# Ten samples' x leave SBUF in layer 1 of a two-layer network; their places take weights of the experts early

## The chip, the cores and the metric

The kernel runs on one core of one Trainium2 chip. The metric is the device time of one execution in microseconds (us), as the median of several runs.

## What is computed

A network of two layers works on x of shape (16, 128, 32, 32), float32: 16 samples, 128 channels, 1024 tokens (pixels). The second layer, around which the change lies, is cut here to what matters:

```
x = x + t_ffn0                          # the end of layer 0: its second residual
x = x + conv_block(_ln_c(x))            # two 3x3 convolutions, relu, residual
t = _to_tokens(x)
u = _ln_t(t)                            # (16, 1024, 128)
logits = einsum('bsd,ed->bse', u, gate_w) + gate_b        # 64 experts
probs  = softmax(logits, axis=1)                          # over the tokens
vals, idx = top_k(probs.transpose(0, 2, 1), 8)            # 8 tokens per expert
pooled = sum over the 8 of gathered u * vals              # (16, 64, 128)
h   = gelu(concat(pooled, 1) @ weight1)                   # per expert, (16, 512)
out = concat(h, 1) @ weight2                              # per expert, (16, 128)
t   = t + scatter_add(out * vals)                         # back to the tokens
```

The experts' weights are 64 matrices of 128 x 512 and 64 of 512 x 128 (and a row of bias each), 33.5 MB in all. SBUF holds only a part of them at a time.

## The kernel before, in words

The kernel first runs layer 0. At its end every sample's x lies in DRAM (`xd[b]`, 512 KB each, written at L634), and the long convolution's spectrum lies in DRAM as `yd`, in two pieces: `yd[0]` with 112 rows and `yd[1]` with 16. The last ones of `yd` are written by `finish` (L828 to L835): four tensor operations on GpSimd (POOL), for the very last on VectorE (DVE), and then the stores on SyncE (SP).

**Layer 1, per sample.** `load(b)` brings x (L974) and the two pieces of y (L977). For sample 0, x and the long piece of y go through POOL's queue, as does the long piece for sample 1; all the others go through SP's. Then class `Routed` has one method for each step: `even`, `odd_t` and so on make z of y; `inverse` (L1074) is a TensorE matmul group that turns y and z back into tokens; `add` (L1081) adds it to x; `tokens`, `stats`, `norm` are the layer norm; `terms`, `image`, `conv` and so on are the two convolutions as a Winograd-like scheme (L958 is the matmul line); `last` (L1219) adds their result to x, in place; `tokens2` transposes x for the second norm; then `logits`, `largest`, `exp`, `replace`, `gates`, `turn`, `pool`, `pooled` are the gating, done once for a pair of samples. `gates` stores the pair's gates in DRAM (`gd`, L1290).

**What sets the order.** A table gives for each step its engine, a cost, a due time, what it needs and which buffers it opens and closes. The function `planned` turns the table into one order of (sample, step). The program emits the steps in this order under `manual_schedule`, with the order pinned on all engines and on SP's queue too. An engine, and SP's queue, works strictly in its order: an instruction that has to wait holds up all behind it on the same engine. y has two buffers, so the y load of a sample waits for the `inverse` of the sample two before.

**Places in SBUF.** Pools are stacked. x of all 16 samples stays in SBUF during layer 1, from the load until the output. Each x is a tile of 4 KB per partition with a tag of its own: x0 in pool `xpool2`, x1 to x15 in `xpool3`.

**The experts.** The weights come in 32 halves of 1 MB: half 2g is the first matrix of the four experts of group g, half 2g+1 the second. `load_half(h)` (L904 ff., the DMAs are L915 for even h and L919 for odd) puts half h into a place of `RING`, a list of nine buffers that layer 1 has finished with (y, wi, z, y, cw0, v, cw1, p1, yo). The first nine halves are issued during the last sample's steps: four behind `inverse`, one behind `convc`, four behind `last`. The gates of the pairs come back from DRAM behind them (L1433, seven loads). Then a loop runs over 16 groups: `hidden(g)` (matmuls L1482 with the weights and L1489 with the bias, GELU on ScalarE (ACT) L1494), `turn` (transposes L1502), `output(g)` (matmuls L1513), `collect` (transpose L1524). Behind `hidden(g)` half 2g+9 is issued, and behind `output(g-1)` half 2g+8: each takes the place of the half that has just been used. In the trace TensorE's instructions of the loop are named by what they write: ph (L1482 and L1489), pht, peo, pot.

**The end.** `big` (L1550), `ob` (L1554), and then for each pair, in the order 0, 1, 2, 3, 7, 4, 5, 6: matmuls pfy (L1572), the add to x (on DVE L1582; for every second sample of the odd pairs a copy on ACT L1579 and the add on POOL L1580), and the store to the output (L1583, 16 stores on SP's queue).

**DMA lanes.** A DMA of SP's queue signals one of eight semaphores in turn; before a DMA is issued, SP also waits for the one eight before it, where it doesn't know yet that it has landed.

Of the kernel before, what the change touches and what calls it, by code (L numbers as in the profile page):

```python
# [8 lines left out]
F32 = mybir.dt.float32  # L9
# [5 lines left out]
P = 128  # L15
B, C, H, W = 16, 128, 32, 32
N = H * W
# [32 lines left out]
E, HID = 64, 512  # L50
# [4 lines left out]
EG = 4  # L55
# [14 lines left out]
def metaformer_kernel(ctx: ExitStack, tc: tile.TileContext, io: dict, out: bass.AP):  # L70
    nc = tc.nc
# [22 lines left out]
    xt = {}  # L94
# [3 lines left out]
    for n, (g_, b_, m_, v_) in enumerate(((V_G1, V_B1, V_M1, V_V1), (V_G2, V_B2, V_M2, V_V2))):  # L98
# [15 lines left out]
                name=nc.get_next_instruction_name(), ins=[], outs=[], act_func_set_id=EXP_LN  # L114
# [52 lines left out]
    with ExitStack() as l0:  # L167
        lconst = l0.enter_context(tc.tile_pool(name="lconst", bufs=1))
        l0.enter_context(tc.issue_after(functions.ins))
        xd = [dram.tile([P, N], F32, name=f"xd{b}", tag=f"xd{b}") for b in range(B)]  # L170
# [23 lines left out]
        for i in range(NF):  # L194
            h = hard[:, i : i + 1]
# [15 lines left out]
        with ExitStack() as a0:  # L211
            aconst = a0.enter_context(tc.tile_pool(name="aconst", bufs=1))
            setup = a0.enter_context(tc.tile_pool(name="setup", bufs=2))
            work = a0.enter_context(tc.tile_pool(name="awork", bufs=2))
# [3 lines left out]
            xpool = a0.enter_context(tc.tile_pool(name="xpool", bufs=8))  # L218
# [85 lines left out]
            def load(b):  # L304
                xt[b] = xpool.tile([P, N], F32, name=f"x{b}", tag="x")
                nc.sync.dma_start(xt[b], xs[b])

            for b in range(2):
                load(b)
# [34 lines left out]
            class Attention:  # L344
# [10 lines left out]
                def tokens(self):  # L355
                    if self.b + 2 < B:
                        load(self.b + 2)
                    self.x = xt[self.b]
                    self.pt = big().rearrange("p (j c) -> p j c", c=C)
                    transpose_in(self.pt, self.x)  # L360
# [384 lines left out]
            samples, setting, preparing = {}, filters(), prepare()  # L745
            with tc.manual_schedule(engines=PINNED):
                for p in range(-reach, B):
                    next(preparing, None)
                    for name, d in period:
                        b = p + d  # L750
# [11 lines left out]
        with ExitStack() as g0:  # L762
# [32 lines left out]
            def collect(c, q, pg):  # L795

                for r in range(RG):
                    dst = gs[c].rearrange("p w (g q i) -> p g q w i", g=RG, q=NB)[:, r, q]
                    src = pg[r].rearrange("p i w -> p w i")
                    if r % 2 and (r == 1 or q % 2 or c == 0):  # L800
                        nc.vector.tensor_copy(dst, src)  # L801
                    else:
                        nc.scalar.copy(dst, src)  # L803
# [87 lines left out]
    with ExitStack() as c1:  # L891

        cconst = c1.enter_context(tc.tile_pool(name="cconst", bufs=1))
        first = c1.enter_context(tc.tile_pool(name="cfirst", bufs=1))
        xpool = [c1.enter_context(tc.tile_pool(name=f"xpool{i}", bufs=1)) for i in (2, 3)]
        work = c1.enter_context(tc.tile_pool(name="cwork", bufs=2))
        cps = c1.enter_context(ExitStack())
        ps = cps.enter_context(tc.tile_pool(name="cps", bufs=2, space=PSUM))

        RING = ("y", "wi", "z", "y", "cw0", "v", "cw1", "p1", "yo")
        FIRST = ("wi", "v", "cw0", "cw1", "p1", "y")
        halves = {}  # L904

        def load_half(h):

            g, n = divmod(h, 2)
            if g >= E // EG:
                return  # L910
            es, tag = slice(g * EG, (g + 1) * EG), RING[h % len(RING)]
            pool = first if tag in FIRST else work
            w = pool.tile([P, EG * HID], F32, name=f"we{n}", tag=tag, bufs=RING.count(tag))
            if n == 0:
                nc.sync.dma_start(  # L915
                    w.rearrange("p (e h) -> p e h", e=EG), w1[es, 0:C, :].rearrange("e d h -> d e h")
                )
            else:
                nc.sync.dma_start(  # L919
                    w.rearrange("p (e i) -> p e i", e=EG),  # L920
                    w2[es, 0:HID, :].rearrange("e (p c) o -> p e (c o)", c=NHC),
                )
            halves[h] = w

        wi = first.tile([P, NQ, 2, P], F32, name="wi", tag="wi")
# [41 lines left out]
        def tokens(t):  # L967
            return t.rearrange("p (j c) -> p j c", c=C)

        yts = {}  # L970

        def load(b):
            xt[b] = xpool[b > 0].tile([P, N], F32, name=f"x{b}", tag=f"x{b}")
            (nc.sync if b else nc.gpsimd).dma_start(xt[b], xd[b])  # L974
            yts[b] = first.tile([P, 2, 2 * NM, C], F32, name="y", tag="y", bufs=2)
            for i, js in enumerate((slice(P - 2 * JL), slice(P - 2 * JL, P))):
                (nc.gpsimd if b < 2 and i == 0 else nc.sync).dma_start(  # L977
                    yts[b][js].rearrange("p r x e -> p r (x e)"),
                    yd[i][:, :, b].rearrange("j r x e -> j r (x e)"),
                )  # L980
# [450 lines left out]
        def load_gates(pr, tag, bufs):  # L1431
            gates[pr] = work.tile([P, N], F32, name=f"gt{pr}", tag=tag, bufs=bufs)
            nc.sync.dma_start(gates[pr], gd[pr])  # L1433
# [5 lines left out]
        with tc.manual_schedule(engines=PINNED | {mybir.EngineType.SP}):  # L1439
            for b in range(2):  # L1440
                load(b)
            for n in range(2):
                nc.sync.dma_start(cw[n], cwd[n])
            nc.sync.dma_start(b1, w1[:, C, :])
            for j in range(2):
                nc.sync.dma_start(b2[j * E : (j + 1) * E, :], w2[:, HID, :])
            samples = [None] * B
            for b, name in order:
                if name == "yin":
                    if b > 1:  # L1450
                        load(b)
                    continue
                if samples[b] is None:
                    samples[b] = Routed(b)
                arg = args.get(name, (name,))
                getattr(samples[b], arg[0])(*(
                    getattr(samples[b], a) if a in ("va", "vb") else a for a in arg[1:]
                ))
                if b == B - 1 and name == "inverse":
                    for h in range(4):  # L1460
                        load_half(h)
                elif b == B - 1 and name == "convc":
                    load_half(4)
                elif b == B - 1 and name == "last":
                    for h in range(5, len(RING)):
                        load_half(h)
                elif b == B - 1 and name == "logits":
                    for pr in range(2):
                        load_gates(pr, "tk", 2)
                    for pr in range(2, 4):  # L1470
                        load_gates(pr, "tt", 4)
# [5 lines left out]
        def hidden(g):  # L1477
            w1t = halves[2 * g].rearrange("p (e h) -> p e h", e=EG)
            ph = ps.tile([P, HID], F32, name="ph", tag="big", bufs=2)
            for i in range(EG):  # L1480
                e = g * EG + i
                nc.tensor.matmul(  # L1482
                    ph[i * CG : (i + 1) * CG, :],
                    pooled[:, e : e + 2, :].rearrange("p e b -> p (e b)"), w1t[:, i, :],
                    start=True, stop=False, skip_group_check=True,
                )
            for i in range(EG):
                e = g * EG + i
                nc.tensor.matmul(  # L1489
                    ph[i * CG : (i + 1) * CG, :], ident[0:E, e : e + 1].to_broadcast([E, CG]), b1,  # L1490
                    start=False, stop=True, skip_group_check=True,
                )
            hs = work.tile([P, HID], F32, name="hs", tag="sa")
            nc.scalar.activation(hs, ph, AF.Gelu)  # L1494
            return hs
# [11 lines left out]
        def output(g, ht):  # L1507
            w2t = halves[2 * g + 1].rearrange("p (e c o) -> p e c o", e=EG, c=NHC)
            po = ps.tile([P, C], F32, name="peo", tag="cv", bufs=3)
            for c in range(NHC):  # L1510
                for i in range(EG):
                    cg = slice(i * CG, (i + 1) * CG)
                    nc.tensor.matmul(  # L1513
                        po[cg, :], ht[:, c, cg], w2t[:, i, c, :],
                        start=(c == 0), stop=(c == NHC - 1), skip_group_check=True,
                    )
            og = work.tile([P, C], F32, name="og", tag="pl", bufs=1)
            nc.vector.tensor_copy(og, po)
            return og
# [10 lines left out]
        with tc.manual_schedule(engines=PINNED):  # L1530
# [4 lines left out]
            for g in range(ng + 1):  # L1535
                if g:
                    ht = turn(hs.pop(g - 1))
                if g < ng:
                    hs[g] = hidden(g)
                    load_half(2 * g + len(RING))  # L1540
                if g > 1:
                    collect(g - 2, og.pop(g - 2))
                if g:
                    og[g - 1] = output(g - 1, ht)
                    load_half(2 * g - 1 + len(RING))
            collect(ng - 1, og.pop(ng - 1))
# [17 lines left out]
        with tc.manual_schedule(engines=PINNED):  # L1564
            yt = first.tile([P, 2, N], F32, name="yt", tag="v")
            for pr in (0, 1, 2, 3, 7, 4, 5, 6):
# [8 lines left out]
                for j in range(2):  # L1575
                    b = 2 * pr + j
# [162 lines left out]
```

## Time and profile before

| | |
|---|---|
| median of 3 runs | 1273.64 us (1272.99 to 1274.5) |
| the profiled execution, its own time | 1271.01 us |
| its span, first to last record | 1269.2 us |
| mean granted TensorE clock in the span | 0.967 |
| TensorE busy | 1149.1 us, 91% |
| VectorE busy | 936.2 us, 74% |
| ScalarE busy | 725.9 us, 57% |
| GpSimd busy | 605.3 us, 48% |
| moved by DMA | 164.64 MB, mean 130 GB/s |
| first inverse of layer 1 (L1074) | at 673.79 us |
| last `last` of layer 1 (L1219, sample 15) | at 1129.87 us |
| first matmul of the experts (L1482) | at 1159.08 us |
| first matmul of the end (pfy, L1572) | at 1240.36 us |
| first output store issued (L1583) | at 1244.59 us |

How to read it: times within the profile count from the start of the span. A busy share is an average over stages with different limits, so the table gives the places of the stages too. SP isn't in the busy list: it only issues DMAs. The duration of a DMA line of SP or POOL is the time of issuing; the transfer itself runs later on the 16 DMA engines, which are shared by all queues. In a timeline row the bracket at the end is the engine's idle time before the row and what ended it. In a table of stretches the columns are: stretch, its length, busy time and count of PE, PEld, DVE, ACT and POOL, the TensorE clock, the DMA engines' mean busy share, and GB/s. PE is TensorE's matmuls, PEld its weight loads.

### The profile page before, as it was taken

To read this page: it belongs to the slowest core of one execution; us is meant where nothing else is said; L and a number is where in the kernel's file an instruction comes from. 1 tells how busy PE (TensorE), PEld (TensorE's weight loads), DVE (VectorE), ACT (ScalarE), POOL (GpSimd) and SP (SyncE) were. 2 spreads that over 40 slices of the span, in tenths; PEclk is the share of its full clock that TensorE was granted. 3 is DMA by queue.
4 is the path that set the end of the run, shared out by engine and by line. 5 is a ranking of instruction groups with operands and counts; after the bars stand their busy time and mean duration, and the time that the engine had idled before them with its cause. 6 is when DMAs were issued, how large, how long until landed. Compare 5 with 4: busy or idle time off the path is not lost. (4 is left out here: it accounts for less than half of the span.)

```text
span 1269.2 us, 34025 instructions
## 1 busy us (share of the span) xinstructions
PE 1149.1 (91%) x14244; PEld 934.4 (74%) x14244; DVE 936.2 (74%) x1944; ACT 725.9 (57%) x1420; POOL 605.3 (48%) x801
## 2 busy tenths in 40 slices
PE   4889999999997999999976999999999999977975
PEld 3677777777776998888865888888898888853432
DVE  5788888888765777776765798889898888772325
ACT  4777777767654777777742354565565556542111
POOL 2335545565666688888863444333353442210002
PEclk9999999999998999999998999999999999985998
DMA  7105343443345244444458231213222212055976
GB/s 264 33 30 165 117 139 124 134 158 111 106 134 183 87 136 137 137 136 136 130 196 244 72 81 34 83 34 84 67 55 77 70 50 101 27 190 190 389 285 265
DMA packets 88346, 164.64 MB, mean 130 GB/s; under 512 B 5632, under 2 KB 41728, under 8 KB 87552
## 3 DMA queue, kind: packets, MB, share of 16 engines
q1 hardware_dynamic: 87312, 159.05, 38.6%
q0 software_dynamic: 880, 3.41, 0.8%
q8 instruction: 112, 1.84, 0.6%
q14 instruction: 42, 0.34, 0.1%
HBM read 105.03 MB, written 57.41 MB: 128 GB/s over the span
## 5 line engine op out<-in xcount | busy, mean ns | idle before, releaser
L958 PE MATMUL pcv<-v,cw 128*128 128x256 f32 x1152 | 259.7, 381 | 0.7 <-POOL v L1144 0.7
L958 PEld LDWEIGHTS pcv<-v,cw 128*128 128x128 f32 x1152 | 215.9, 191 | 34.3 <-issue 4.9
L801 DVE COPY g<-pg 128x512 f32<-128x512 f32 x196 | 127.8, 682 | 77.1 <-PE pg L790 77.1
L803 ACT COPY g<-pg 128x512 f32<-128x512 f32 x316 | 161.2, 605 | 31.7 <-PE pg L790 30.9
L790 PE MATMUL pg<-ph,mst 32*128 32x128 f32 x4096 | 139.6, 278 | 5.0 <-issue 3.5
L790 PEld LDWEIGHTS pg<-ph,mst 32*128 32x128 f32 x4096 | 126.0, 186 | 19.1 <-issue 12.4
L814 PE MATMUL py<-g,v 128*32 128x128 f32 x4096 | 127.9, 276 | 8.5 <-POOL v L781 5.7
L814 PEld LDWEIGHTS py<-g,v 128*32 128x32 f32 x4096 | 110.1, 111 | 18.3 <-POOL v L781 5.8
L144 ACT ACTIVATE tok<-tok,sts 128x128 f32<-128x128 f32 x256 | 101.9, 480 | 16.8 <-DVE sts L1031 13.4
L135 DVE BATCH_NORM_STATS2 bst<-big 128x6 f32<-128x256 f32 x256 | 91.1, 416 | 23.3 <-PE big L152 14.1
L781 POOL TENSOR_TENSOR v<-xc 128x256 f32<-128x256 f32 x128 | 99.8, 803 | 8.9 <-DMA xd<-x 8.9
L626 PE MATMUL big<-u,mu 128*128 128x128 f32 (+4 forms) x384 | 86.0, 380 | 0.0
L1144 POOL TENSOR_TENSOR v<-abss 128x256 f32<-128x256 f32 x64 | 49.1, 788 | 66.1 <-DVE abss L1140 54.3
L277 POOL TENSOR_TENSOR xf<-ab 128x256 f32<-128x256 f32 x34 | 24.8, 729 | 112.3 <-DVE ab L244 112.3
L1163 POOL TENSOR_TENSOR yo<-abss 128x256 f32<-128x256 f32 x32 | 23.5, 736 | 109.1 <-DVE abss L1159 109.1
L626 PEld LDWEIGHTS big<-u,mu 128*128 128x128 f32 x384 | 56.7, 191 | 18.0 <-issue 15.4
L875 ACT COPY yt<-py 128x512 f32<-128x512 f32 x64 | 37.5, 586 | 48.9 <-PE py L814 26.4
L1580 POOL TENSOR_TENSOR x<-yt,x 128x1024 f32<-128x1024 f32 x4 | 9.4, 2359 | 115.2 <-ACT yt L1579 115.2
L559 PE MATMUL big<-wf,ub 128*128 128x256 f32 x256 | 62.0, 385 | 0.2
L144 ACT ACTIVATE tt<-tt,sts 128x128 f32<-128x128 f32 x128 | 51.1, 481 | 14.6 <-DVE sts L1031 14.6
L152 PEld LDWEIGHTS big<-ident,x 128*128 128x128 f32 x384 | 46.0, 146 | 17.7 <-issue 10.5
L782 POOL TENSOR_SCALAR v<-v 128x256 f32<-128x256 f32 x64 | 55.2, 862 | 5.6
(247 smaller groups left out, 2480.5 us busy)
## 6 DMA issues: line engine op xcount, KB each, us to landing
we<-in_weight SPq DMA_DIRECT2D x32, 1024.0 KB, 9.9
vd<-xf SPq DMA_DIRECT2D x16, 1024.0 KB, 5.1
xc<-vd SPq DMA_DIRECT2D x64, 256.0 KB, 3.2
yd<-ys SPq DMA_DIRECT2D x32, 512.0 KB, 4.0
y<-yd SPq DMA_DIRECT2D x14, 896.0 KB, 6.7
x<-in_x SPq DMA_DIRECT2D x16, 512.0 KB, 4.6
mi<-in_M_phi SPq DMA_DIRECT2D x16, 512.0 KB, 4.7
xd<-x SPq DMA_DIRECT2D x16, 512.0 KB, 6.1
```

The source lines that it names most:

```text
L135: nc.vector.bn_stats(bst[:, j : j + 2, :].rearrange("p j s -> p (j s)"), src[:, j : j + 2, :].rearrange("p j c -> p c j"),)
L144: nc.scalar.activation(dst[:, j, :], src[:, j, :], AF.Identity, bias=nm[:, j : j + 1], scale=r[:, j : j + 1],)
L559: nc.tensor.matmul(dst, self.ub[:, q, :], wf[:, q, :], start=True, stop=True)
L626: nc.tensor.matmul(self.pa[:, a:hi], mu[:, NF - 1 - si, tap, :], self.u[:, a - tap : hi - tap], start=(tap == 0), stop=(tap == KU - 1),)
L781: nc.gpsimd.tensor_tensor(vv[:, x, 1:, bs], e, o, op)
L782: nc.gpsimd.tensor_scalar(v[:, :, 0, bs], v[:, :, 2, bs], -1.0, None, ALU.mult)
L790: nc.tensor.matmul(pg[r][:, i], mst[rs, 4 * q + i, :], ph[rs, c, :], start=True, stop=True,)
L801: nc.vector.tensor_copy(dst, src)
L803: nc.scalar.copy(dst, src)
L814: nc.tensor.matmul(py[rows, x, kl, :], v[:, (x * NM + m) * JL + jl, 1 - ri : 3 - ri, :] .rearrange("p k b -> p (k b)"), g[:, ((x * 2 + ri) ...
L958: nc.tensor.matmul(pc[:, i], wt[:, dy, k, :], v[:, k, dy * WT : dy * WT + HT], start=(dy == 0), stop=(dy == 2),)
L1144: nc.gpsimd.tensor_tensor(v[:, k, WT : WT + HT], self.ab[:, 0], self.ab[:, 1], op)
```

## The change

x of two samples becomes one tile: `xp0` to `xp7`, 8 KB per partition, all in the pool `xpool2`. The x of pairs 1 to 5 (samples 2 to 11) no longer stays in SBUF: behind `tokens2` of each of these samples x is stored to its place in DRAM, `xd[b]`, through SP's queue. The ring gets five more places, `xp1` to `xp5`, ahead of the nine old ones. Halves 0 to 4 go into them: half 0 is issued behind `tokens2` of sample 4, half 1 behind that of sample 6, and so on to half 4 behind that of sample 12. The nine old places take halves 5 to 13 at the same points of the last sample as before. In the experts' loop half 2g+14 is issued behind `hidden(g)` and half 2g+13 behind `output(g-1)`. When the 32 halves have all been issued, the next five calls of `load_half` bring the ten samples' x back from DRAM, a pair at a time, into the places that come next in the ring; the end then adds to these tiles and stores them.

```diff
-        xpool = [c1.enter_context(tc.tile_pool(name=f"xpool{i}", bufs=1)) for i in (2, 3)]
+        xpool = c1.enter_context(tc.tile_pool(name="xpool2", bufs=1))
...
-        RING = ("y", "wi", "z", "y", "cw0", "v", "cw1", "p1", "yo")
+        AWAY = range(1, 6)
+        RING = tuple(f"xp{pr}" for pr in AWAY) + (
+            "y", "wi", "z", "y", "cw0", "v", "cw1", "p1", "yo",
+        )
...
             g, n = divmod(h, 2)
+            es, tag = slice(g * EG, (g + 1) * EG), RING[h % len(RING)]
             if g >= E // EG:
+                pr = AWAY[0] + h - 2 * (E // EG)
+                if pr in AWAY:
+                    tag = RING[(pr - AWAY[0] + 18) % len(RING)]
+                    pool = first if tag in FIRST else xpool if tag[:2] == "xp" else work
+                    x = pool.tile([P, 2, N], F32, name=f"xb{pr}", tag=tag, bufs=RING.count(tag))
+                    for j in range(2):
+                        xt[2 * pr + j] = x[:, j]
+                        nc.sync.dma_start(x[:, j], xd[2 * pr + j])
                 return
...
         def load(b):
-            xt[b] = xpool[b > 0].tile([P, N], F32, name=f"x{b}", tag=f"x{b}")
+            if b % 2 == 0:
+                xp[b // 2] = xpool.tile([P, 2, N], F32, name=f"xp{b // 2}", tag=f"xp{b // 2}")
+            xt[b] = xp[b // 2][:, b % 2]
             (nc.sync if b else nc.gpsimd).dma_start(xt[b], xd[b])
...
+                if name == "tokens2":
+                    if b // 2 in AWAY:
+                        nc.sync.dma_start(xd[b], samples[b].x)
+                    if b % 2 == 0 and b // 2 - 1 in AWAY:
+                        load_half(b // 2 - 1 - AWAY[0])
                 if b == B - 1 and name == "inverse":
-                    for h in range(4):
+                    for h in range(5, 9):
                         load_half(h)
                 elif b == B - 1 and name == "convc":
-                    load_half(4)
+                    load_half(9)
                 elif b == B - 1 and name == "last":
-                    for h in range(5, len(RING)):
+                    for h in range(10, len(RING)):
                         load_half(h)
```

More of the change, by code (lines that the diff above doesn't have):

```diff
@@ L908, in load_half @@
             g, n = divmod(h, 2)
+            es, tag = slice(g * EG, (g + 1) * EG), RING[h % len(RING)]
             if g >= E // EG:
+                pr = AWAY[0] + h - 2 * (E // EG)
[6 more added lines that the diff above has]
+                        nc.sync.dma_start(x[:, j], xd[2 * pr + j])
                 return
-            es, tag = slice(g * EG, (g + 1) * EG), RING[h % len(RING)]
-            pool = first if tag in FIRST else work
+            pool = first if tag in FIRST else xpool if tag[:2] == "xp" else work
             w = pool.tile([P, EG * HID], F32, name=f"we{n}", tag=tag, bufs=RING.count(tag))
@@ L968, in tokens @@
             return t.rearrange("p (j c) -> p j c", c=C)
-        yts = {}
+        yts, xp = {}, {}
         def load(b):
-            xt[b] = xpool[b > 0].tile([P, N], F32, name=f"x{b}", tag=f"x{b}")
+            if b % 2 == 0:
+                xp[b // 2] = xpool.tile([P, 2, N], F32, name=f"xp{b // 2}", tag=f"xp{b // 2}")
+            xt[b] = xp[b // 2][:, b % 2]
             (nc.sync if b else nc.gpsimd).dma_start(xt[b], xd[b])
```

## The prediction

> **What bounds the kernel now.** I first read the slices of the page, for the stretch in which the weights move:
>
> ```profile
> PE   4889999999997999999976999999999999977975
> ...
> PEclk9999999999998999999998999999999999985998
> DMA  7105343443345244444458231213222212055976
> ```
>
> A slice is 31.7 us. From 760 to 1100 us (slices 24 to 34) TensorE is busy in nine tenths and the DMA engines in one to three: layer 1 is bound by TensorE and leaves the DMA nearly free. In the last slices this turns round. Next the chain of waits, for the experts (from 1159 us):
>
> ```profile
> 1199.74 0.99 PE ph L1482 x8
> 1200.74 13.77 DMA we<-in_weight
> ...
> 1216.11 13.81 DMA we<-in_weight
> 1229.92 0.04 issue
> 1229.96 1.06 PE ph L1482 x8
> ```
>
> Up to 1200 us the chain is TensorE's, then weight loads. TensorE's timeline shows what that costs (start, duration; in brackets the idle time before):
>
> ```profile
> 1195.73 1.06 PE L1482 MATMUL ph<-we,pooled 128*32 128x512 f32 x8
> 1199.67 1.06 PE L1482 MATMUL ph<-we,pooled 128*32 128x512 f32 x8
> ...
> 1209.17 1.06 PE L1482 MATMUL ph<-we,pooled 128*32 128x512 f32 x8 [1.35 <-DMA we<-in_weight]
> 1214.55 1.06 PE L1482 MATMUL ph<-we,pooled 128*32 128x512 f32 x8 [1.38 <-DMA we<-in_weight]
> 1219.53 1.06 PE L1482 MATMUL ph<-we,pooled 128*32 128x512 f32 x8 [0.98 <-DMA we<-in_weight]
> 1224.83 1.06 PE L1482 MATMUL ph<-we,pooled 128*32 128x512 f32 x8 [1.29 <-DMA we<-in_weight]
> 1229.96 1.06 PE L1482 MATMUL ph<-we,pooled 128*32 128x512 f32 x8 [1.13 <-DMA we<-in_weight]
> ```
>
> One group of four experts takes 3.94 us while TensorE is full (the steps 1176.05, 1179.98 ... 1199.67: 23.62 us for six). The last six, from 1199.67 to 1229.96, take 30.29 us. The loads cost 30.29 - 23.62 = 6.67 us. Last, the stretches of 5 us behind it (busy times of PE, PEld, DVE, ACT, POOL; clock; DMA share; GB/s):
>
> ```profile
> 1215.00:1220.00 5.00, 4.02 (x59) 1.82 (x53) 1.26 (x3) 0.60 (x1) 0.00 (x0) 1.00 1.05 408
> 1225.00:1230.00 5.00, 3.87 (x57) 1.70 (x51) 1.26 (x3) 0.60 (x1) 0.00 (x0) 1.00 0.72 276
> 1230.00:1235.00 5.00, 4.33 (x63) 2.10 (x67) 1.43 (x4) 0.60 (x1) 0.00 (x0) 1.00 0.01 2
> 1235.00:1240.00 5.00, 2.26 (x41) 1.56 (x32) 2.41 (x10) 0.00 (x0) 0.00 (x0) 1.00 0.00 0
> 1240.00:1245.00 5.00, 4.64 (x14) 2.06 (x16) 1.98 (x4) 0.00 (x0) 0.00 (x0) 0.66 0.00 0
> 1255.00:1260.00 5.00, 2.72 (x12) 0.94 (x8) 3.91 (x4) 1.01 (x1) 3.76 (x2) 1.00 1.02 419
> ```
>
> The DMA engines are full up to the last weight, idle from 1230 to 1245 us, then full again with the 16 outputs (8.4 MB at 419 GB/s, 20 us). So the end is three limits in a row: weights by DMA, the rest of the experts by TensorE (10.4 us from the last ph at 1229.96 to the first pfy at 1240.36), outputs by DMA (28.9 us from there to the end of the span).
>
> [...] what the tail moves takes its bytes over about 0.40 MB per us. [...] every added DMA holds SP's queue until its wait is met. [...] SP's timeline has such gaps (27.4 us ahead of L919). [...] the gaps here are at most 1.4 us and the clock stays 1.00, so ending them buys the gaps alone.
>
> **The change, part by part.** I compared the built order of both kernels. PE, DVE and ACT keep their order; two waits on weights fall away on PE early and two later. New are ten stores, five early weight halves, ten reloads, and one wait on POOL.
>
> *Five halves early.* In the stage from 1161 us on, 23 halves were loaded; now 18, as 14 instead of 9 lie ready. A half is 1.05 MB, 2.62 us at 0.40 MB/us. The releases are the old ones, so loads start at the same time. Counted in MB units from 1161 us the new queue is 18 weights and five pairs of x: 23 again, so its end stays near 1229.9 us. Half 30, for the last ph, is the 16th: 1229.9 - 7 x 2.62 = 1211.6, needed at 1199.67 + 23.62 = 1223.3. Half 31 is the 19th: 1219.4, needed near 1228 (its peo stands 4.8 us behind that ph). Nothing is late; TensorE keeps 3.94 us to the end. **-6.67 us.** What is late next is TensorE itself, then the outputs.
>
> *Ten reloads of x* (5.24 MB, 13.1 us of DMA). The SP queue has pair 1 ahead of half 31, pairs 3, 2, 5, 4 behind it. Their places come free by about 1211 us (ph of the twelfth group, peo of the eleventh). They end near 1230; the first pfy moves to 1233.7 and the first add, 3.0 us behind it, to 1236.7. They fill the DMA's old idle time: **0**, margin 6.8 us. Without that cover up to 13.1 us. Outputs wait for stores and DMAs long landed.
>
> *Ten stores of x and five loads in layer 1* (10.5 MB). Each store waits on SP for `last` of its sample (L1219, 16 of them, 1.97 us). In SP's timeline the queue's next item is a y load that waits anyway for the inverse of two samples before. For sample 3: last ends at 820.7 us, behind the store stands x of sample 9 (issued at 814.25, needed only at its add some 80 us later) and then y at 837.7. For sample 4: 846.1, next the gates' store at 858.6. The pattern repeats every 56 us; the last one, sample 11 at 1045.0, stands ahead of a weight load of 1036.7, a delay of 8.3 us for something needed near 1178. An even y loaded at 812.5 is first read at 840.6, so DMA contention has 20 us of room; the DMA share there is 0.13 to 0.32. A load's wait for two stores is met: the later was issued 25 us ahead. **0**; a bound from above is 10 issues of 1.75 us (the median of the old xd stores), 17.5 us, if nothing hid them, but SP is idle there for most of the time.
>
> *POOL's x0 load.* x0 now shares a tile with x1, whose place comes free with the last matmul of layer 0 (L814, ends 657.52). Before:
>
> ```profile
> 652.92 0.61 POOL L974 DMA_DIRECT2D x<-xd  x1
> 653.56 1.29 POOL L829 TENSOR_TENSOR ys<-ys 128x512 f32<-128x512 f32 x1
> 654.78 0.72 POOL L977 DMA_DIRECT2D y<-yd  x1
> ...
> 656.21 0.73 POOL L831 TENSOR_TENSOR ys<-ye 128x256 f32<-128x256 f32 x1
> 656.88 0.71 POOL L977 DMA_DIRECT2D y<-yd  x1
> 673.98 0.95 POOL L990 TENSOR_TENSOR z<-y 128x256 f32<-128x256 f32 x1 [16.39 <-DMA y<-yd]
> ```
>
> In the new order L829 to L831 come first (2.76 us, to 655.7), then the wait, then x0 at 657.5, y of sample 0 at 658.2 and of sample 1 at 658.9: 3.4 and 2.0 us later than before. Queued behind: the z of POOL, and through it the first inverse of TensorE. But y lands 9.9 us after issue, at 668.1, and z waited to 673.98 for the other piece of y, which SP issues at 670.33 when the last ys stores have landed. These stores share the DMA engines with the 2.36 MB moved later: at worst +3.4 us. Below nothing: SP's first store waits for L831, which ends 1.2 us earlier: -1.2. [...] both ends stay in the range; I take **0**.
>
> *Sum:* -6.67 us. The profiled execution took 1271.01 us (span 1269.2 and 1.8 around it), 2.6 us under the median of the runs, 1273.64. Taken from the median: 1273.64 - 6.67 = **1267.0 us**.
>
> **The rivals.**
> A, *the new wait at the start of layer 1 counts*: POOL's loads crowd SP's last ys stores, and all of layer 1 starts up to 3.4 us later. For: the DMA share is 0.9 or more from 652 to 668 us. Against: [...] that this is nearly the same work in the same time. 1267.0 + 3.4 = 1270.4 us.
> B, *TensorE doesn't hold its pace*: filled to the end, it gets a lower clock, so 34 us (from 1199.7 to 1233.7) at 0.85 cost 6.0 us. For: the clock isn't always 1.00 (0.967 over the span). Against: 340 us of layer 1 at 98% busy run at 1.00. 1273.0 us: no change.
> C, *slower: the reloads are slow*. Four pairs (4.2 MB) start at 1219.4 behind half 31. The end moves with theirs once they pass 1240, where the outputs then begin to move (1246 in the trace); the gain is gone at 1246.7, which is 27 us for 4.2 MB, or 150 GB/s. At 120 GB/s they end at 1254: 1267.0 + 14 = 1281 us. For: no stretch has them alone. Against: outputs and y with packets of the same 4 KB go at 400 GB/s.
> That the change doesn't do what it says is excluded by the built order: the loads stand in SP's queue as described.
>
> **How the numbers follow.** Forecast 0.76 (its own range 1265 to 1269, for -1.2 at the start and 2 us of spread), A 0.11, B 0.07, C 0.06. The range takes the forecast and A: 1264.5 to 1270.8. A measurement of this kernel can tell about 0.2%, 2.5 us, from no change, so faster means under 1271.1: forecast and most of A, 0.85; same 0.09; slower C, 0.06.
>
> **What would show it.** Right: ph starts every 3.94 us to the last, near 1223; no wait for we behind 1200; the DMA near 400 GB/s to about 1230; pfy near 1234; outputs 28.9 us from there; the first inverse at 673 to 675 us. Wrong: an idle time ahead of ph, a DVE or POOL add that waits for x<-xd, a later first inverse, or a last sample of layer 1 that ends later than 1158 us.

## The result, and the profile after

| | before | after |
|---|---|---|
| median of 13 runs each, same comparison | 1276.89 us (1272.53 to 1284.12) | 1264.80 us (1259.31 to 1271.15) |
| ratio, 95% interval | | 0.9904 (0.9883 to 0.9924) |
| the profiled execution, its own time | 1271.01 us | 1271.15 us |
| its span | 1269.2 us | 1269.4 us |
| its mean clock | 0.967 | 0.965 |

The kernel is faster by 12.1 us in the medians; the interval makes it 9.7 to 14.9 us. The forecast was 6.7 us and 1267.0 us. The two profiled executions, however, end at the same time. That of after is the longest of its 13 runs, that of before is shorter than all 13 of its own. So the two traces can be compared stage by stage, but not by their ends. First the slices of the page of after:

```profile
PE   4889999999997999999994999999999999986995
...
PEclk8999999999998999999997999999999999996998
DMA  7105343443336344444448423233233223245996
```

In layer 1 (slices 24 to 34) the DMA digits are two to three where they were nought to three, and TensorE's stay at nine. TensorE's timeline of after, first the start of the experts, then their end:

```profile
1166.45 1.94 PE L1500 MATMUL ph<-we,pooled 128*32 128x512 f32 x8 [0.38 <-DVE pooled L1338]
1172.02 1.94 PE L1500 MATMUL ph<-we,pooled 128*32 128x512 f32 x8
1178.68 1.69 PE L1500 MATMUL ph<-we,pooled 128*32 128x512 f32 x8
1183.24 1.06 PE L1500 MATMUL ph<-we,pooled 128*32 128x512 f32 x8
...
1222.61 1.06 PE L1500 MATMUL ph<-we,pooled 128*32 128x512 f32 x8
...
1226.55 1.07 PE L1500 MATMUL ph<-we,pooled 128*32 128x512 f32 x8
...
1230.48 1.07 PE L1500 MATMUL ph<-we,pooled 128*32 128x512 f32 x8
```

No bracket names we any more, and the last groups keep 3.94 us (1222.61, 1226.55, 1230.48). From the first ph to the last it is 64.03 us; before it was 70.88 (1159.08 to 1229.96). The loads' share is gone: -6.85 us. The stretches of 5 us of after show what filled the DMA's old idle time:

```profile
1225.00:1230.00 5.00, 5.00 (x86) 2.69 (x81) 1.56 (x5) 0.99 (x2) 0.00 (x0) 1.00 1.03 420
1230.00:1235.00 5.00, 4.60 (x58) 2.24 (x57) 1.96 (x5) 0.60 (x1) 0.00 (x0) 1.00 0.98 399
1235.00:1240.00 5.00, 2.50 (x41) 1.81 (x41) 2.28 (x10) 0.00 (x0) 0.00 (x0) 1.00 0.09 35
1240.00:1245.00 5.00, 4.12 (x12) 1.84 (x14) 1.64 (x5) 0.00 (x0) 0.00 (x0) 0.66 0.00 0
1255.00:1260.00 5.00, 3.56 (x14) 1.31 (x14) 4.41 (x4) 1.01 (x1) 4.29 (x2) 1.00 1.02 414
```

The reloads of x run at 399 to 420 GB/s and are done some 5 us ahead of the first pfy at 1240.88. Last, POOL at the start of layer 1 of after:

```profile
661.91 0.90 POOL L831 TENSOR_TENSOR ys<-ye 128x256 f32<-128x256 f32 x1
666.21 0.62 POOL L987 DMA_DIRECT2D xp<-xd  x1 [3.40 <-PE py L814]
666.83 1.36 POOL L990 DMA_DIRECT2D y<-yd  x2
682.05 0.96 POOL L1003 TENSOR_TENSOR z<-y 128x256 f32<-128x256 f32 x1 [13.87 <-DMA y<-yd]
```

The wait for layer 0's last matmul is there: 3.40 us. Where did the profiled execution of after lose what it won? In layer 0, in code that both kernels share: POOL's memset of p at the end of layer 0 stands at 650.66 us in the trace of before and at 657.40 in that of after.

So two things were open: what the other 5 us of the measured 12.1 are, and whether the new wait costs anything. One trace is one execution, and the 13 executions of one kernel differ by up to 12 us here; each experiment below therefore gives one more trace as well as its times. This table holds the stages of all traces, in us, from their timelines:

| trace | memset of p to first z | first inverse to end of the last `last` | from there to first ph | first ph to last ph | first pfy to end |
|---|---|---|---|---|---|
| before | 23.3 | 458.0 | 27.3 | 70.9 | 28.8 |
| before again | 23.3 | 458.9 | 27.2 | 70.6 | 28.6 |
| before_warm | 23.0 | 461.8 | 24.3 | 67.2 | 28.2 |
| before_cold | 22.3 | 458.6 | 35.2 | 70.9 | 29.7 |
| x0_alone | 24.9 | 457.3 | 27.4 | 64.3 | 28.3 |
| best_warm_x0 | 23.1 | 456.1 | 26.3 | 58.9 | 27.8 |
| pairs_k0 | 27.4 | 458.5 | 26.1 | 68.9 | 29.1 |
| away_k2 | 24.5 | 457.6 | 26.2 | 61.7 | 35.6 |
| away_k3 | 26.9 | 458.4 | 26.6 | 58.8 | 29.9 |
| after | 24.7 | 457.4 | 27.2 | 64.0 | 28.5 |
| after again | 25.9 | 458.0 | 26.0 | 58.9 | 28.3 |
| after_warm | 25.0 | 458.3 | 23.7 | 58.9 | 27.8 |
| after_cold | 24.2 | 458.4 | 34.2 | 61.6 | 28.9 |
| no_x_traffic | 26.4 | 457.5 | 27.1 | 64.0 | 29.0 |

In the first six POOL's load of x0 has no wait, in the other eight it has.

### The profile page after: what moved, and what is told of

Same layout as the page of the kernel before. It is cut to its first block, busy times and chain, and to the rows that moved or that the text cites. A ratio compares the mean times of both kernels' runs of the same rounds, so it can differ in the third digit from the quotient of the medians.

```text
span 1269.4 us, 34066 instructions
## 1 busy us (share of the span) xinstructions
PE 1149.6 (91%) x14244; PEld 934.4 (74%) x14244; DVE 934.9 (74%) x1944; ACT 726.0 (57%) x1420; POOL 603.9 (48%) x801
## 5 line engine op out<-in xcount | busy, mean ns | idle before, releaser
L144 ACT ACTIVATE tok<-tok,sts 128x128 f32<-128x128 f32 x256 | 101.9, 480 | 16.8 <-DVE sts L1044 13.4
L277 POOL TENSOR_TENSOR xf<-ab 128x256 f32<-128x256 f32 x34 | 24.7, 727 | 114.0 <-DVE ab L244 113.9
L1598 POOL TENSOR_TENSOR xb<-yt,xb 128x1024 f32<-128x1024 f32 x3 | 7.1, 2353 | 107.6 <-ACT yt L1597 107.6
L464 POOL TENSOR_TENSOR ke<-ke,ks 128x1024 f32<-128x1024 f32 x16 | 30.6, 1913 | 55.7 <-DVE qs L472 44.1
```

What stands on the lines that cost most here:

```text
L144: nc.scalar.activation(dst[:, j, :], src[:, j, :], AF.Identity, bias=nm[:, j : j + 1], scale=r[:, j : j + 1],)
```

## The experiments

**Both kernels again.** No edit.

> The kernel before, unchanged, for a second trace of it. The measured step from before to after is 12.1 us in the medians, but the two profiled executions end within 0.2 us of each other: the trace of after lost 6.7 us in layer 0, in code that both kernels share, and won 6.85 us in the experts. Theory 1 (chance in layer 0): the experts' stretch from the first ph to the first pfy is 81.3 us again, within 1 us, and the executions differ in layer 0. Theory 3 (the weight loads are slower in other executions of the kernel before): the stretch is well above 81.3 us, up to 87, since the kernel before waits for loads at its end and the kernel after doesn't. Ratio to before: 1.000.

> The kernel after, unchanged, for a second trace of it. Experts' stretch from the first ph to the first pfy 74.4 us again under every theory, since TensorE is full there. Theory 1: ratio to before 0.995 in the long run, and the measured 0.990 was partly chance. Theory 2 (something in layer 0 or at the start of layer 1 is faster in the kernel after, which the first trace doesn't show because of chance): ratio 0.990, the first inverse of layer 1 earlier than in the traces of before. Theory 3: ratio 0.990, no earlier first inverse.

Measured: before again 1275.57 us, ratio 1.0017 (0.9997 to 1.0038); after again 1263.63 us, ratio 0.9922 (0.9896 to 0.9948). The step is there again. Theory 3 falls: before waits for loads as in its first trace (81.0 us from the first ph to the first pfy, 70.6 of them to the last ph). Theory 2 falls: the first inverse isn't earlier in after. Theory 1 alone doesn't do either, for the experts' stretch of after again isn't 74.4 us but 69.3, and for a reason that none of the three had named. Its timeline, at the start of the experts:

```profile
1162.30 1.07 PE L1500 MATMUL ph<-we,pooled 128*32 128x512 f32 x8 [0.38 <-DVE pooled L1338]
1166.32 1.07 PE L1500 MATMUL ph<-we,pooled 128*32 128x512 f32 x8
1170.00 1.07 PE L1500 MATMUL ph<-we,pooled 128*32 128x512 f32 x8
1173.94 1.06 PE L1500 MATMUL ph<-we,pooled 128*32 128x512 f32 x8
```

The same first ph takes 1.07 us here and 1.94 in the trace of after. The first three groups take 11.6 us (1162.30 to 1173.94) instead of 16.8 (1166.45 to 1183.24). The stretches of both show why; first after, then after again (the clock is the third number from the end):

```profile
1165.00:1170.00 5.00, 4.14 (x19) 0.58 (x17) 0.64 (x2) 3.73 (x9) 0.00 (x0) 0.50 0.74 219
1170.00:1175.00 5.00, 4.28 (x24) 1.13 (x20) 0.69 (x1) 0.60 (x1) 0.00 (x0) 0.50 0.56 201
1175.00:1180.00 5.00, 5.00 (x48) 2.32 (x44) 0.98 (x2) 0.60 (x1) 0.00 (x0) 0.50 0.80 249
```

```profile
1155.00:1160.00 5.00, 3.90 (x31) 3.50 (x31) 0.00 (x0) 1.01 (x1) 0.00 (x0) 0.50 0.09 35
1160.00:1165.00 5.00, 3.50 (x29) 1.16 (x25) 0.65 (x2) 3.74 (x10) 0.00 (x0) 0.88 0.58 194
1165.00:1170.00 5.00, 4.36 (x57) 2.24 (x57) 0.98 (x2) 1.19 (x2) 0.00 (x0) 1.00 0.90 289
```

In the gating of the last pair TensorE waits for the other engines (gaps of 4.35 and 5.55 us in both traces). Its granted clock is 1.00 ahead of the first gap (from 1139 to 1143 us in after, 1136 to 1140 in after again), then 0.50 (1147 to 1151) and 0.55 (1144 to 1148), and behind the second gap 0.50 in both (1159 to 1163, 1156 to 1160). When it comes back differs between executions of one program: before the first ph in after again, 13 us after it in the first trace of after. The two differ by some 14 us, counted from the first ph, and in the trace of after TensorE worked without a gap for 9 us (1170.97 to 1180) before the clock came back; what sets the moment, neither trace shows. This gave theory 4: **a start at half clock costs the kernel after 5 us, and the kernel before, which waits for loads at the end anyway, less.** What the change is worth then depends on the clock at the start.

**The tiles of two samples alone.** No x is stored or reloaded; the ring keeps its nine places, and the loads stand where they stood in before.

```diff
-        AWAY = range(1, 6)
+        AWAY = range(1, 1)
```

> The tiles of two samples and the wait of POOL's load of x0 that comes with them, alone: no x is stored, no half is loaded early, no x reloaded (the ring has its nine old places). The prediction gave this part 0, between -1.2 and +3.4 us. Theory 1 and 3: ratio 1.000 (0.999 to 1.001), the experts' stretch as in before. Theory 2, if the faster part is the start of layer 1: ratio near 0.996.

Measured: 1271.98 us, ratio 0.9994 (0.9974 to 1.0014): no gain without the early halves, so the gain is theirs. This trace started near full clock and shows the loads' side of theory 4 (timeline, TensorE):

```profile
1164.78 1.07 PE L1500 MATMUL ph<-we,pooled 128*32 128x512 f32 x8 [0.38 <-DVE pooled L1338]
...
1205.52 1.07 PE L1500 MATMUL ph<-we,pooled 128*32 128x512 f32 x8 [1.12 <-DMA we<-in_weight]
1210.88 1.06 PE L1500 MATMUL ph<-we,pooled 128*32 128x512 f32 x8 [1.36 <-DMA we<-in_weight]
...
1227.56 1.07 PE L1500 MATMUL ph<-we,pooled 128*32 128x512 f32 x8 [2.33 <-DMA we<-in_weight]
1230.77 1.94 PE L1531 MATMUL peo<-we,ht 128*32 128x128 f32 x32
...
1233.69 1.93 PE L1500 MATMUL ph<-we,pooled 128*32 128x512 f32 x8
```

The first three groups are 5 us quicker, but the last ph comes only 2 us sooner after the first (68.9 us against 70.9). Of the other 3.4 us, the waits for weights take something over 1 (their brackets add up to 7.4 us; in the trace of before to 6.1). The larger part looks like the clock again: behind the last wait, of 2.33 us, the next peo took 1.94 us instead of 1.08 and the last ph 1.93 instead of 1.07, the durations that the trace of after has at a clock of 0.50. The step to the last ph took 6.13 us instead of 3.94, without a wait for weights.

**Three pairs, two pairs.** The same line, with the load positions moved along, and the buffer yt of the end in xp1.

```diff
-        AWAY = range(1, 6)
+        AWAY = range(1, 4)      # away_k2: range(1, 3)
...
-            yt = first.tile([P, 2, N], F32, name="yt", tag="v")
+            yt = xpool.tile([P, 2, N], F32, name="yt", tag="xp1")
```

> Three pairs away in place of five (three early halves, six stores, six reloads; the buffer yt of the end takes the place of xp1). By the arithmetic of the prediction half 30 then lands at 1216.8 and is needed at 1223.3, so three early halves do what five do: theory 1: the experts' stretch 74.4 us and the same time as the kernel after (ratio of the two 1.000). Theory 3 with slow loads: part of the gain is missing, up to 3 us more than after.

> Two pairs away (two early halves, four stores and reloads). By the arithmetic of the prediction every early half takes one load, 2.62 us, from the queue ahead of half 30. Starting from 70.7 us (cold) or 67.2 to 68.9 us (warm) from the first ph to the last: 65.5 us cold (the floor there is 64.0), 62.0 to 63.7 us warm (the floor is 58.9): a part of the waits for weights is left. Rival (the early halves act in another way than by bytes in the queue): 58.9 or 64.0 us as with three and five.

Measured: three pairs 1263.21 us, ratio 0.9906 (0.9875 to 0.9937), 58.8 us from the first ph to the last, no wait for weights: three early halves do what five do. Two pairs: 61.7 us, with waits ahead of the last two groups only:

```profile
1211.61 1.06 PE L1500 MATMUL ph<-we,pooled 128*32 128x512 f32 x8
1216.90 1.06 PE L1500 MATMUL ph<-we,pooled 128*32 128x512 f32 x8 [1.28 <-DMA we<-in_weight]
1222.28 1.07 PE L1500 MATMUL ph<-we,pooled 128*32 128x512 f32 x8 [1.37 <-DMA we<-in_weight]
```

Both start near full clock (first ph 1.06 and 1.07 us). So does before_warm (below; 1.06 us), with no early half, no half clock further on and 67.2 us. From there two early halves take off 5.5 us, or 2.8 us each, by one trace each, where the arithmetic had 2.62; three reach 58.8 us, the floor of TensorE's own work. The 68.9 us of pairs_k0 aren't used for this, for 2.2 of them are the half clock of its last group. The time of away_k2 as a whole (1275.59 us, ratio 0.9994, 0.9973 to 1.0014) says nothing on this: its end is 35.6 us long, because my edit put yt into xp1, where with a ring of eleven places the reload of pair 2 lands. ScalarE waited for that pair's output:

```profile
1247.60 1.93 ACT L1597 COPY yt<-pfy 128x1024 f32<-128x1024 f32 x2 [22.26 <-DMA out<-xb]
```

**Clock held up.** Ten matmuls, whose result nobody reads, in TensorE's idle times of the last gating, in both kernels.

```diff
+        def warm(n):
+            d = ps.tile([P, HID], F32, name="warm", tag="cv", bufs=3)
+            for _ in range(n):
+                nc.tensor.matmul(d, ident[0:E, :], b1, start=True, stop=True)
...
+        WARM = {(B - 3, "pooled"): 4, (B - 1, "logits"): 5, (B - 1, "turn"): 1}
...
+                if (b, name) in WARM:
+                    warm(WARM[b, name])
```

> The kernel after with ten idle-time matmuls on TensorE in the gating of the last pair (the bias matrix b1 into a free PSUM tile, read by nobody: four ahead of the last channels, five behind the last logits, one behind the last turn). Theory 4: in the traces the first three groups of the experts take 17.0 us where the granted clock is 0.5 at their start and 11.6 us where it is 1.0; the kernel after, bound by TensorE, keeps the 5.2 us of difference to its end. With TensorE kept busy every execution starts at 1.0: first ph to last ph 58.9 us, the end of last to the first ph 23 to 25 us where it was 26.0 to 27.2, and 3 to 7 us less than the kernel after: ratio to before near 0.986. Rival (the gain of 12 us has nothing to do with the clock): same time as after, 0.991, or a little more for the added matmuls.

> The kernel before with the same ten matmuls. Theory 4: its weight loads bound the end, so a warm start is worth less in the experts' stretch: first ph to last ph 68.9 us (as in the trace of the pairs alone, which started warm) where it was 70.7, and the steps ahead of the first ph get 2 to 3 us shorter as in the kernel after: ratio 0.996 to 0.998. Rival: 1.000.

Measured: after_warm 1261.99 us, ratio 0.9884 (0.9856 to 0.9911); before_warm 1268.28 us, ratio 0.9926 (0.9899 to 0.9953). In the traces the first ph takes 1.07 and 1.06 us (in after_warm the clock is 0.60 from 1144 to 1148 us and 1.00 from there on), the stretches are 58.9 and 67.2 us, and the way to the first ph is 3 us shorter in both. Both got faster, and before_warm by 8.9 us in the medians where its trace explains 6.6 (2.9 ahead of the first ph, 3.7 in the stretch) and I expected 3 to 5. Between the two, 6.3 us in the medians are left to everything else that the change does (95% interval 0 to 11, by resampling the six executions of each); the traces give 8.3 in the stretch.

**Clock held down.** Twelve VectorE operations ahead of the last pooled_copy, so that TensorE idles for 8.3 to 8.5 us, in both kernels.

```diff
+                if (b, name) == (B - 1, "pooled_copy"):
+                    for _ in range(12):
+                        nc.vector.tensor_scalar(samples[b].gtt, samples[b].gtt, 1.0, None, ALU.mult)
```

> The kernel after with twelve operations on VectorE (a tile that is no longer needed, times one, some 0.73 us each) ahead of the last pooled_copy, so that TensorE stands idle for about 9 us ahead of the first ph and every execution should start the experts at half clock. Theory 4: first ph to last ph 64.0 us, about 5 us more than in the kernel after_warm; the whole is 9 us longer than after for the idle time, and again up to 5 us for the executions that would have started warm. Rival (the clock isn't what differs): 58.9 or 64.0 us by chance as before.

> The kernel before with the same twelve operations. Theory 4: first ph to last ph 70 to 71 us as in the two cold traces (the halves that lie ready have longer to land, but the nine places are the same), and the difference of after_cold to before_cold is the loads' 6.7 us alone, ratio 0.995, against some 8 to 9 us between after_warm and before_warm. Rival: the difference of the cold pair is the measured 11 to 12 us, too.

Measured: after_cold 1274.94 us, ratio 0.9990 (0.9969 to 1.0010); before_cold 1283.97 us, ratio 1.0072 (1.0046 to 1.0097). Their difference is 9.0 us (6.5 to 11.9, by the same resampling), more than the 6.7 expected. The traces have 61.6 and 70.9 us, a difference of 9.3, and a first ph of 1.94 and 1.93 us. The idle time didn't do fully what it should: in after_cold the first two groups took 5.58 and 4.83 us and the third 3.94, so the clock came back one group sooner than in the trace of after (5.57, 6.66, 4.56). A start in between, then, and a gain in between; before_cold stayed at 70.9. By the traces the expectation of 6.7 fails; the times alone, whose interval reaches down to 6.5, can't exclude it. That the stretch follows the start clock holds.

**x0 in its own place.**

```diff
-        xpool = c1.enter_context(tc.tile_pool(name="xpool2", bufs=1))
+        xpool0 = c1.enter_context(tc.tile_pool(name="xpool2", bufs=1))
+        xpool = c1.enter_context(tc.tile_pool(name="xpool3", bufs=1))
...
+            if b < 2:
+                xt[b] = (xpool if b else xpool0).tile([P, N], F32, name=f"x{b}", tag=f"x{b}")
...
```

> The kernel after with x0 in a tile and a pool of its own again, so that POOL's load of x0 has no wait; all else as in after. In the traces the time from the last matmul of layer 0 to the first inverse is 16.3 and 15.8 us for the kernel before and 16.2, 16.3, 18.4 and 18.0 us with the wait. If the wait costs what rival A said: 15.8 to 16.3 us here and 1 to 2 us less than after in all (ratio to before 0.990). If it costs nothing: 16 to 18 us here too and the same time as after.

Measured: 1265.92 us, ratio 0.9915 (0.9893 to 0.9936); against after, nothing can be told. The measure I had named (last matmul of layer 0 to the first inverse, 17.9 us here) was a bad one, since the wait also orders POOL's work ahead of it. Counted from POOL's memset of p, six traces without the wait have 22.3 to 24.9 us to the first z, mean 23.3, and eight with it 24.2 to 27.4, mean 25.6. **By the stages the wait costs some 2.3 us**, an estimate from these means; the ranges touch at one trace, x0_alone itself, so the size is not better known than to about 1 us. SP's queue shows where it arises, first before, then after:

```profile
656.97 7.67 SPq L835 DMA_DIRECT2D yd<-ys  x4
670.33 0.64 SPq L977 DMA_DIRECT2D y<-yd  x1
```

```profile
662.84 7.21 SPq L835 DMA_DIRECT2D yd<-ys  x4
678.53 0.64 SPq L990 DMA_DIRECT2D y<-yd  x1
```

From the end of issuing the last four ys stores to the next load of y it is 5.7 us before and 8.5 after. In before_warm, x0_alone and best_warm_x0, without the wait too, it is 5.6, 7.4 and 5.4; in after again, with it, 8.4. The times don't show this cost: pairs_k0, which has the wait and not the early halves, differs from before by -0.8 us in its ratio (-3.3 to +1.8), and x0_alone, without the wait, is no faster than after. The section on the sum has a likely reason, the clock.

**No traffic of x.** The stores and the reloads are left out, and the tiles are set to zero instead.

```diff
+                    nc.gpsimd.memset(x, 0.0)
...
-                        nc.sync.dma_start(x[:, j], xd[2 * pr + j])
...
-                    if b // 2 in AWAY:
-                        nc.sync.dma_start(xd[b], samples[b].x)
```

> The kernel after without the stores of ten samples' x and without their reloads: the tiles that the end adds to are set to zero by POOL instead, so the output of samples 2 to 11 lacks x. The prediction gave this traffic 0: same time as after, ratio to before 0.991, and the same stretches of layer 1 (458 us from the first inverse to the end of the last last). If the 10.5 MB cost something: up to 3 us less in layer 1, or a shorter end.

Measured: 1260.22 us, ratio 0.9878 (0.9846 to 0.9909), an interval that overlaps those of after (0.9904 and 0.9922). The trace shows no place where the traffic would cost: layer 1 takes 457.5 us against 457.4 and 458.0, the experts 64.0 as in the trace of after, the end 29.0. Six runs of it lie between 1257.2 and 1270.4, so the 3 to 6 us less than after, by the ratios, can be the start clock; I count the traffic as 0 by the stages, not by the times.

**A faster candidate.** x0 alone, the ten matmuls, and three more of them ahead of the last sample's.

```diff
+        WARM = {(B - 3, "turn"): 2, (B - 2, "channels"): 1, (B - 3, "pooled"): 4, (B - 1, "logits"): 5, (B - 1, "turn"): 1}
```

> A candidate for a faster kernel: after, with x0 in its own tile and pool, and with thirteen idle-time matmuls (the ten of after_warm, two behind the turn of the last pair but one and one behind the channels of sample 14) so that the last logits run at full clock, too. First ph to last ph 58.9 us, the end of last to the first ph near 22 us (logits at 1.9 us instead of 4.2), ratio to before 0.985 to 0.988.

Measured: 1259.90 us, ratio 0.9882 (0.9849 to 0.9915), the lowest median that computes all of the output, with after_warm beside it (0.9884); their intervals overlap with that of after, so they are the best candidates, not shown to be faster than it. The way to the first ph was 26.3 us, not 22: the added matmuls didn't hold the clock through the gating. It was 0.77 in the 4 us from 1144, with the last logits, and 0.57 in those from 1156, with the last pool, and came back (1.00 from 1160) just ahead of the first ph:

```profile
1143.69 3.56 PE L1278 MATMUL big<-tk,gw 128*64 128x512 f32 x8
1147.18 4.55 PE L1457 MATMUL warm<-b,ident 64*128 64x512 f32 x10
1152.80 1.94 PE L152 MATMUL big<-ident,eg 128*128 128x128 f32 x8 [1.07 <-DVE rs L1305]
...
1156.67 3.31 PE L1325 MATMUL pp<-tt,gtt 128*64 128x128 f32 x32
...
1161.18 1.07 PE L1513 MATMUL ph<-we,pooled 128*32 128x512 f32 x8 [0.38 <-DVE pooled L1342]
```

## Why the prediction was right, and where it was not

**The end of the experts: right in mechanism, right for one execution, too small for the others.** The profile of after shows -6.85 us where the sum had -6.67; ph keeps its 3.94 us, no load is waited for, and three early halves are enough, as half 30's arithmetic implied (11.7 us to spare with five, 6.5 with three). What was mis-sized is that term: it took the trace's first three groups, 17.0 us, as given. They ran at half clock in that execution. The kernel before loses 3 to 4 us by that, since its loads set the end: 70.6 to 70.9 us against the 67.2 of before_warm. The kernel after loses 5: 64.0 against 58.9. So the term is 6.3 to 6.9 us where both start at half clock, 8.3 where both start near full clock, and 9.3 in the pair held down, where after got its clock back earlier than before. That the gaps are all that a wait for weights costs, because the clock stays at 1.00, was right for the trace of before, but not in general: by its durations pairs_k0 lost 2.2 us more at half clock behind a wait of 2.33 us, where the waits in the trace of before were at most 1.38.

**The reloads: right.** They ended near 1235 us, 5 us ahead of the first pfy; the forecast had 3.7. The end is 28.3 and 28.5 us, as before. Rival C is out: they ran at 399 to 420 GB/s.

**The stores and early loads in layer 1: right.** SP's timeline of after has the stores directly behind the `last` they wait for, and the next y loads at their old distance. For sample 3, whose `last` ends at 827.46, and its followers:

```profile
827.49 0.33 SPq L1474 DMA_DIRECT2D xd<-xp  x1
827.86 0.43 SPq L987 DMA_DIRECT2D xp<-xd  x1
844.44 1.21 SPq L990 DMA_DIRECT2D y<-yd  x2
852.88 0.33 SPq L1474 DMA_DIRECT2D xd<-xp  x1
853.31 0.39 SPq L926 DMA_DIRECT2D we<-in_weight  x1
```

Layer 1 lasts 457.4 us against 458.0.

**POOL's x0 load: wrong, as the stages show; rival A was right in kind.** I took 0 between -1.2 and +3.4; the traces say about +2.3. The failed part of the step is my estimate that SP's last ys stores lose nothing beside POOL's 2.36 MB: with the wait the next load of y stood 8.4 and 8.5 us behind their issue, in the four traces without it 5.4 to 7.4. POOL waited 2.0 to 4.7 us in the eight traces where I had 1.8, and SP could issue the second piece of y for sample 0 only 21.1 and 22.3 us after the memset of p in the two traces of after (678.53 and 674.85), against 19.7 before (670.33).

**B** is out: the clock was 1.00 from 1180 us to the last group. The clock mattered, but ahead of the stretch that I looked at.

**The sum.** 1267.0 us was forecast and 1264.8 measured. That they lie so near is in part luck: the median of before is 1276.89 us in this comparison, 3.3 us above the one that I started from, and the step is 5.4 us larger than forecast. The two misses go opposite ways.

The stages give -6.3 to -8.3 us in the experts and +2.3 at the start of layer 1, so -4.0 to -6.0 where both kernels start the experts at the same clock, and up to some 11 us where after starts near full clock and before at half (70.7 to 58.9 us, 1.2 ahead of it, less the 2.3). With the clock steered in both, the medians differ by 6.3 and 9.0 us, with the wide intervals given above. The kernels as they are gave 12.1 (9.7 to 14.9) and 9.9 us (6.6 to 13.2).

What makes up the rest is shown in part. Each kernel has one or two traces, but the mean granted clock of every execution is on record. On the chip of pairs_k0 and after again it was 0.9618 on average over 47 executions of before, 0.9661 over 17 of after and 0.9669 over 22 of pairs_k0. For each 0.001 that the mean clock of an execution was lower, it took 0.6 us longer in before, 0.7 in pairs_k0 and 0.9 in after. An estimate from straight lines through these executions: at equal clock after is some 6 us faster than before, pairs_k0 some 3 us slower than before, and after some 9 us faster than pairs_k0. (The same fit puts the second set of executions of before, 14 of them, 1.4 us from the 47, so none of these is better known than to 1 to 2 us.) This fits the stages: the early halves win 8 to 9, the wait costs 2 to 3, and some 3 us of the step from before to after again are the higher clock. It also fits that pairs_k0 and x0_alone show no cost of the wait in their times: pairs_k0 had the higher clock, and x0_alone, with 0.962 over six executions on another chip, the lower one. Among the traces that nothing steers, before, before again and x0_alone, without the wait, start the experts at half clock; of the six with it, four start near full clock. So, by this estimate, the 6.7 us of the forecast are about the net step at equal clock, by two errors that cancel: the experts win more, and the wait isn't free. A mean doesn't tell where in the execution the clock was low, and why it was higher in the kernels with the wait stays open.

## What to carry to other kernels

A stage that waits for DMA hides part of the losses ahead of it: a half-clock start cost 3 to 4 us here with the waits and 5 without them. Size a gain from several traces, not from one execution's waits, and compare the clock of the executions as well as their times. Count bytes in the queue ahead of the last thing needed: three early loads were worth as much as five (58.8 and 58.9 us from the first ph to the last). Merging two tiles into one makes the earlier load wait for the later place (2.0 to 4.7 us here); look at what stands behind that load in its queue, and at what it then moves beside.

## What the runs showed that I had not expected

The granted clock can stay at 0.50 for 13 us after the experts' start although TensorE is busy 4.3 to 5.0 of every 5 us (1170 to 1180 us in the trace of after), and in other executions of the same program it is back at their start. Matmuls put into the idle time to hold it up don't do it surely: the logits of best_warm_x0 took 3.56 us, starting 3.8 us behind 3.70 us of such matmuls, against 1.94 us for the logits of an earlier pair in the trace of after (at 1081.26, clock 1.00). Layer 0, the same code in all kernels, reached its end (the memset of p) anywhere between 648.4 and 657.4 us.
